# A four-layer graph network on one core: the third layer aggregates plain features by Strassen products and multiplies by its matrix afterwards

## The chip, the cores and the metric

The kernel runs on one core of a Trainium2 chip. The metric is the device time of one execution in microseconds (us). The median of three runs before the change is 2856.06 us (2855.82 to 2856.15). Engines are named as in the profile: PE (matrix engine; PEld is its weight load), DVE (vector), ACT (scalar), POOL (gpsimd) and SP (sync, which issues transfers). "Clock" is the share of its full clock that PE was granted.

## What is computed

A graph has 4096 nodes with 256 features each and one adjacency matrix (int32, symmetric in its pattern, with ones on the diagonal). Four layers follow one another, and each is wrapped as `x = layernorm(x + layer(x))`.

```
layer 0: additive attention, 4 heads of 64, leaky relu 0.2, softmax over neighbours, ELU
layer 1: 4-head dot-product attention over neighbours (Wq, Wk, Wv with biases)
layer 2: h = x @ W
         e[i,j] = leaky_relu(h[i]·a[:D] + h[j]·a[D:], 0.01), only where adj[i,j] > 0
         elu(softmax_j(e) @ h)
layer 3: cosine attention: unit vectors of x @ Wq.T and x @ Wk.T (128 wide), exp, mask, softmax,
         0.5 * (softmax @ x) + 0.5 * x
```

"Third layer" here is layer 2 of this list, the one with a single additive head. Two identities matter. Softmax times `h` is softmax times `x`, times `W`, so the matrix can come before or after the sum over neighbours. And the exponential of a leaky relu of a sum is the greater of two products of a factor of the row and a factor of the column, so no exponential is needed for each pair of nodes: before, the kernel writes it as `(relu(row * dst - 1) + 1) * mask`, up to factors that cancel in the softmax or are put into the values.

## The kernel before

All features stay in `X`, 32 tiles of 128 nodes (`NT`), each 256 wide. Attention is computed transposed: neighbours lie on the partitions, and a block of 512 nodes (`QW`; `NB` = 8 blocks, `QB` = 4 tiles in each) on the columns. Every layer loops over the blocks, and within a block over the neighbours. The orders of PE, and in layer 1 of DVE and ACT too, are those of the program text (`manual_schedule`); in the third layer only PE's order is fixed, and the framework's scheduler orders DVE and ACT.

Layer 1 (`multi_head_attention`) goes over 64 units of 64 neighbours in each block (`NH`). `scores` loads a mask on SP's queue for each four units, makes four 64x64-weight products into one of three `p` buffers in PSUM (L670), and exponentiates them on ACT (L672). `weights` multiplies with the mask on DVE (L682), from PSUM into one of eight `prob` buffers. The denominators are summed beside that: even units are added to `den` by POOL (L689), odd units by a DMA that accumulates, issued from POOL's queue (L695). `sums` is the product with the values (L703), three units later. The function `finish(b, j)` does a part of the finishing of the block before after unit j of the sums: it joins the three parts of `den` on DVE at j = 7 and 9 (L712), turns, divides, adds to `X`, takes mean and variance (j = 21 to 27) and the inverse root of the variance (j = 29 on DVE, `end_root` at j = 31 on POOL, L156 to L159), and scales the rows (`scale_row`, j = 35 to 41). The last block is finished by `tail`, inside the third layer.

The third layer (`additive_one`) first turns `X` block by block on PE (L118), projects with the matrix and the two attention columns (`additive_values`, L200), and keeps `V`, `src`, `dst` and a `row` of 4096 column factors; all this lies before and between the sums of block 0. For each tile of neighbours, `weights` makes `e` on ACT (L460) and `prob` on DVE (L462), with both inputs in SBUF. `sums` has four products of 128 weight columns of `prob` with the 257 columns of `V` (L468). A block's results are taken from PSUM by `take_all` (L474, L476); `outputs` and `add_elu` (L214 to L217) finish it over the next block, and `layernorm_block` with `lift=True` prepares the next layer. In the last block the cosine layer's `prepare` (L883 and on) turns and projects the finished blocks.

The last layer (`cosine_attention`) has scores (L941), exponentials (L945), mask products (L952) and mixes of weights (L954 to L957) for pairs of tiles, and already multiplies a 2x2 arrangement of half features and half blocks with seven products in place of eight (`product`, L966). `parts` joins the sum of one `acc` tile of four banks on ACT and DVE (L972 to L984) before the turns on PE (L992).

The function `turned_apart` turns a block by DVE's 32x32 transposes (L131) and a round trip through DRAM, without PE.

Of the kernel before, what the change touches and what calls it, by code (L numbers as in the profile page):

```python
# [9 lines left out]
FP = mybir.dt.float32  # L10
# [11 lines left out]
QB = 4  # L22
# [6 lines left out]
def kernel(  # L29
# [49 lines left out]
    X = feat.tile([P, NT, D + 1], FP, name="X")  # L79
    nc.vector.memset(X[:, :, D:], 2.0)  # L80
# [42 lines left out]
    def turned_apart(squares, far, part, to, eng):  # L123

        B = P // QB
        squares = squares.tile([P, QB, KC, P], FP, name="squares")
        far = far.tile([QB, B, QB, KC * P], FP, name="far")
        for c in range(KC):  # L130
            nc.vector.transpose(squares[:, :, c, :].rearrange("p q (k n) -> p k q n", n=B),  # L131
                                part(c).rearrange("p k (q f) -> p k q f", f=B))
        eng.dma_start(far.rearrange("a f q m -> (a f) (q m)"), squares.rearrange("p q c m -> p (q c m)"))
        for q in range(QB):
            eng.dma_start(to[q * B:(q + 1) * B], far[:, :, q, :].rearrange("a f m -> f a m"))
        return to.rearrange("p a (c m) -> p c a m", c=KC)

    def block_apart(sb, once, dr, b, eng):
        xT = sb.tile([P, KC * QW], FP, name="xT").rearrange("p (a m) -> p a m", a=QB)
        return turned_apart(once, dr, lambda c: X[:, b * QB:(b + 1) * QB, c * P:(c + 1) * P], xT, eng)  # L140
# [34 lines left out]

    def normalise(ys, mv, lift=False):
        v, r, n = begin_root(mv)
        end_root(v, r, n)
        if lift:

            nc.vector.tensor_tensor(v, v, r, OP.mult)
            nc.vector.tensor_tensor(mv[:, :, 0], mv[:, :, 0], v, OP.subtract)
        for k, y in enumerate(ys):
            scale_row(y, mv, r, k)
# [25 lines left out]
    def add_elu(o, b, k, mv):  # L210

        y = X[:, b * QB + k, :D]
        neg = fin1.tile([P, D], FP, name="neg")
# [6 lines left out]
    def additive_heads(a, H, slope, early, narrow, ahead):  # L220
# [7 lines left out]
        with ExitStack() as lay:  # L228
# [83 lines left out]
            def outputs(po, b, k):  # L312
                rden = fin.tile([P, H], FP, name="rden")
                nc.vector.reciprocal(rden, po[:, HC, ::G])
                o = fin.tile([P, D], FP, name="o")
# [3 lines left out]
                add_elu(o, b, k, mvs[b])  # L319

            def finish(b, j):
# [6 lines left out]
                if j in (4, 7, 10, 13):  # L328
                    k = (j - 4) // 3
                    outputs(pos[b, k], b, k)  # L330
# [67 lines left out]
        def tail(bank):  # L398
            b = NB - 1
            for k in range(QB):  # L400
                outputs(turned(bank, b, k), b, k)
# [3 lines left out]
    def additive_one(w_sb, slope, tail, op, follow):  # L405

        MJ = 2
        mvs, taken = {}, {}
        with ExitStack() as lay:
            keep = pool(lay, "gb_keep", 1)  # L410
            V = keep.tile([P, NT, D + 1], FP, name="V")
            src = keep.tile([P, NT, 1], FP, name="src")
            dst = keep.tile([P, NT, 1], FP, name="dst")
            row = keep.tile([P, N], FP, name="row")
            zp = pool(lay, "gb_z", 3)
            sb = pool(lay, "gb_sb", 2)
            xp = pool(lay, "gb_turn", 3)
            sq = pool(lay, "gb_squares", 1)
            far = pool(lay, "gb_far", 2, space=bass.MemoryType.DRAM)

            follow.turning = xp, sq, far
            mp = pool(lay, "gb_mask", 4)
            dr = pool(lay, "gb_dram", 2, space=bass.MemoryType.DRAM)

            ps = pool(lay, "gb_ps", 4, space=PSUM)
            pa = pool(lay, "gb_pa", 1, space=PSUM)
            edges = adjT.rearrange("(t p) i -> p t i", p=P)
            mask, acc, prob = {}, {}, {}
# [4 lines left out]
            def turn(b):  # L433
                return transposed_block(xp, bank, b)

            def project(b, xT, ks=range(QB)):
                groups = [(k, 1, bank().rearrange("p (n f) -> p n f", n=1)) for k in ks]
                additive_values(xT, b, groups, w_sb, V, src, dst, 1, slope)

            def fill_row(b):  # L440
                part = row[:, b * QW:(b + 1) * QW]
                if b > 1:

                    far = dr.tile([QB, P], FP, name="far")
                    nc.gpsimd.dma_start(far.rearrange("k p -> p k"), src[:, b * QB:(b + 1) * QB, 0])
                    nc.gpsimd.dma_start(part, far.rearrange("k p -> (k p)").unsqueeze(0).to_broadcast([P, QW]))
                    return
                pr = bank()
                for k in range(QB):
                    nc.tensor.transpose(pr[:, k * P:(k + 1) * P], src[:, b * QB + k, :].to_broadcast([P, P]), ident)  # L450
                nc.scalar.copy(part, pr)

            def weights(b, j):
                cols = slice(b * QW, (b + 1) * QW)
                m = b, j // MJ
                if j % MJ == 0:
                    mask[m] = mp.tile([P, MJ, QW], I32, name="mask")
                    nc.sync.dma_start(mask[m], edges[:, j:j + MJ, cols])
                e = sb.tile([P, QW], FP, name="e")
                nc.scalar.activation(e, row[:, cols], AF.Relu, bias=-1.0, scale=dst[:, j, :])  # L460
                prob[b, j] = zp.tile([P, QW], FP, name="prob")
                nc.vector.scalar_tensor_tensor(prob[b, j], e, 1.0, mask[m][:, j % MJ, :], OP.add, OP.mult)  # L462

            def sums(b, j):
                if j == 0:
                    acc[b] = [bank() if b % 2 else pa.tile([P, QW], FP, name=f"acc{k}") for k in range(QB)]
                for k in range(QB):
                    nc.tensor.matmul(acc[b][k][:, :D + 1], prob[b, j][:, k * P:(k + 1) * P], V[:, j, :],  # L468
                                     start=(j == 0), stop=(j == NT - 1))

            def take_all(b):
                for k in range(QB):
                    rden = fin.tile([P, 1], FP, name="rden1")
                    nc.vector.reciprocal(rden, acc[b][k][:, D:D + 1])  # L474
                    taken[b, k] = op.tile([P, D], FP, name="o")
                    nc.vector.tensor_scalar_mul(taken[b, k], acc[b][k][:, :D], rden)  # L476

            def outputs(b, k):
                if k == 0:
                    mvs[b] = fin.tile([P, QB, 2], FP, name="mv")  # L480
                add_elu(taken[b, k], b, k, mvs[b])
                if k == QB - 1:
                    layernorm_block(b, mvs[b], lift=True)

            def even_bank():
                n = next(even) % QB
                return pa.tile([P, QW], FP, name=f"acc{n}")

            even = itertools.count()
            units = [(b, j) for b in range(NB) for j in range(NT)]  # L490
            with tc.manual_schedule(engines={mybir.EngineType.PE}):
                xTs = {0: turn(0), 1: turn(1)}
                project(0, xTs[0])
                project(1, xTs[1], [0, 1])
                fill_row(0)
                project(1, xTs[1], [2, 3])
                for i in range(len(units) + 1):
                    if i < len(units):
# [691 lines left out]
```

## Time and profile before

| | us |
|---|---|
| median of three runs | 2856.06 |
| profiled execution: time | 2856.27 |
| profiled execution: span on the core | 2854.5 |
| PE busy | 2832.5 (99%) |
| DVE, ACT, POOL busy | 2168.0, 1653.4, 945.3 |
| layer 0 | 0 to 722.5 |
| layer 1: projections; blocks | to 809; to 1709.6 |
| third layer | to 2213 |
| cosine layer; end | to 2842; to 2854.5 |

The granted clock was 0.998 over the span. The span is the time from the first to the last instruction on the core; the device time is 1.8 us longer. The borders of the layers are read from the lines that PE works on. In the profile a group is one line, engine, operation and tile; "mean ns" is the mean length of one instruction, which for pipelined matmuls is longer than the distance from one start to the next. "Idle before" is the time in which the engine had nothing to do just ahead of that group, with what ended it.

### The profile page before, as it was taken

What the parts mean: (1) busy time and instruction counts of PE and PEld (TensorE: products, weight loads), DVE (VectorE), ACT (ScalarE), POOL (GpSimd) and SP (SyncE); (2) the same over time, 40 slices, a digit from 0 to 9 for tenths busy, and PEclk for the clock granted to TensorE, in tenths of its full rate; (3) what the DMA queues carried; (4) which work ended last, traced back from release to release, by engine and by line L of the source; (5) the groups of instructions that cost most, each with busy time, mean ns of one, the idle gap of its engine ahead of it and who ended that gap; (6) DMA issues with size and microseconds to landing.
All of it is one profiled execution on the core that took longest, in us unless ns stands there. A gap on an engine that the chain in (4) does not pass through costs nothing.

```text
span 2854.5 us, 50462 instructions
## 1 busy us (share of the span) xinstructions
PE 2832.5 (99%) x19905; PEld 1503.5 (53%) x19905; DVE 2168.0 (76%) x2913; ACT 1653.4 (58%) x2590; POOL 945.3 (33%) x705
## 2 busy tenths in 40 slices
PE   9999999999999999999999999999999999999998
PEld 4333333333543333333333338888888777777775
DVE  8899999999677777777777775565557966666665
ACT  8899999998256666666666664444445322222222
POOL 0001001010058889899899891000002000000000
PEclk9999999999999999999999999999999999999999
DMA  7566767665359899899899895655558544444441
GB/s 209 104 136 139 140 136 140 133 136 106 97 112 195 178 191 191 181 193 187 183 193 185 186 183 126 174 165 175 158 159 221 104 65 61 61 66 59 62 57 29
DMA packets 237088, 398.04 MB, mean 139 GB/s; under 512 B 20929, under 2 KB 121265, under 8 KB 235954
## 3 DMA queue, kind: packets, MB, share of 16 engines
q0 software_dynamic: 104320, 184.06, 40.5%
q1 hardware_dynamic: 132112, 210.36, 24.9%
q8 instruction: 156, 2.56, 0.4%
q14 instruction: 82, 0.67, 0.1%
q10 hardware_dynamic: 418, 0.40, 0.0%
HBM read 328.60 MB, written 32.58 MB: 127 GB/s over the span
## 4 chain that ended last, share of the span: by engine, by line
PE 97%; DVE 2%; ACT 0%; issue 0%; DMA 0%; ACTq 0%
PE acc L297 23%; PE p L670 15%; PE acc L703 15%; PE acc L966 13%; PE acc L468 8%; PE g L468 8%; PE p L941 3%; PE g L941 3%; PE g L585 2%; PE g L200 1%; PE pv L604 1%; PE acc L883 1%; PE acc L200 1%; PE g L118 1%; PE g L309 0%; DVE prob L952 0%
## 5 line engine op out<-in xcount | busy, mean ns | idle before, releaser
L682 DVE TENSOR_TENSOR prob<-p,mask 128x1024 f32<-128x1024 f32 x512 | 623.9, 1223 | 209.3 <-ACT p L672 203.2
L672 ACT ACTIVATE p<-p,shift 128x1024 f32<-128x1024 f32 x512 | 556.2, 1088 | 325.2 <-PE p L670 324.4
L297 PE MATMUL acc<-prob,V 128*32 128x512 f32 x6144 | 664.0, 592 | 1.2 <-DVE prob L287 1.2
L689 POOL TENSOR_TENSOR den<-den,prob 128x1024 f32<-128x1024 f32 x248 | 625.6, 2522 | 74.9 <-DVE prob L682 67.1
L284 ACT ACTIVATE prob<-row,dst 128x512 f32<-128x512 f32 x1020 | 633.2, 713 | 0.1
L287 DVE SCALAR_TENSOR_TENSOR prob<-prob,mask 128x2048 f32<-128x2048 f32 x256 | 582.5, 2287 | 24.2 <-ACT prob L284 21.5
L670 PE MATMUL p<-qT,kT 64*64 64x512 f32 x4096 | 532.3, 590 | 0.8 <-DVE prob L682 0.8
L703 PE MATMUL acc<-prob,V 64*64 64x512 f32 x4096 | 531.5, 589 | 0.0
L297 PEld LDWEIGHTS acc<-prob,V 128*32 128x32 f32 x6144 | 197.3, 110 | 453.0 <-issue 431.7
L91 POOL COPY tick<-prob 128x1 f32<-128x1 f32 x35 | 40.0, 1143 | 992.8 <-DVE prob L287 643.9
L460 ACT ACTIVATE e<-row,dst 128x512 f32<-128x512 f32 x256 | 183.9, 721 | 247.2 <-DVE prob L462 218.5
L703 PEld LDWEIGHTS acc<-prob,V 64*64 64x64 f32 x4096 | 155.9, 133 | 285.3 <-issue 278.1
L462 DVE SCALAR_TENSOR_TENSOR prob<-e,mask 128x512 f32<-128x512 f32 x256 | 177.2, 694 | 165.9 <-PE acc L468 88.5
L670 PEld LDWEIGHTS p<-qT,kT 64*64 64x64 f32 x4096 | 154.4, 133 | 277.3 <-issue 261.6
L952 DVE TENSOR_TENSOR prob<-prob,mask 128x1024 f32<-128x1024 f32 x128 | 156.4, 1222 | 165.9 <-ACT prob L945 165.8
L695 POOL DMA_DIRECT2D den<-prob x240 | 228.9, 954 | 14.7 <-DVE prob L682 6.7
L868 POOL DMA_DIRECT2D mask<-in_adjT x64 | 47.5, 742 | 538.7 <-DVE prob L952 424.8
L468 PE MATMUL acc<-V,prob 128*128 128x257 f32 x1024 | 225.1, 380 | 0.0
L468 PE MATMUL g<-V,prob 128*128 128x257 f32 x1024 | 223.7, 380 | 0.0
L468 PEld LDWEIGHTS g<-V,prob 128*128 128x128 f32 x1024 | 194.3, 190 | 27.7
L468 PEld LDWEIGHTS acc<-V,prob 128*128 128x128 f32 x1024 | 193.6, 190 | 27.6 <-issue 0.4
L966 PE MATMUL acc<-mix,mixed 128*128 128x256 f32 x768 | 206.9, 379 | 0.0
(199 smaller groups left out, 2520.8 us busy)
## 6 DMA issues: line engine op xcount, KB each, us to landing
mask<-in_adjT SPq DMA_DIRECT2D x256, 512.0 KB
den<-prob POOLq DMA_DIRECT2D x240, 512.0 KB, 5.1
mask<-edges SPq DMA_DIRECT2D x512, 64.0 KB
mask<-in_adjT POOLq DMA_DIRECT2D x64, 512.0 KB, 5.7
edges<-in_adj POOLq DMA_DIRECT2D x32, 512.0 KB, 10.1
far<-squares SPq DMA_DIRECT2D x16, 512.0 KB
den<-prob SPq DMA_DIRECT2D x16, 512.0 KB
row<-far SPq DMA_DIRECT2D x7, 1024.0 KB
```

What stands on the lines that cost most here:

```text
L284: nc.scalar.activation(z[:, h, :], r, AF.Relu, bias=-1.0, scale=dst[:, j, h:h + 1])
L287: nc.vector.scalar_tensor_tensor(z, z, 1.0, mask[m][:, j % MJ, :].unsqueeze(1).to_broadcast([P, H, QW]), OP.add, OP.mult)
L297: nc.tensor.matmul(acc[b][h * G:(h + 1) * G, n, :], part, prob[b, j][:, h, :], start=(j == 0), stop=(j == NT - 1))
L460: nc.scalar.activation(e, row[:, cols], AF.Relu, bias=-1.0, scale=dst[:, j, :])
L468: nc.tensor.matmul(acc[b][k][:, :D + 1], prob[b, j][:, k * P:(k + 1) * P], V[:, j, :], start=(j == 0), stop=(j == NT - 1))
L670: nc.tensor.matmul(p[c * d:(c + 1) * d, r, :], kT[half, c, at:at + d], qT[half, c, cols], start=True, stop=True)
L672: nc.scalar.activation(p, p, AF.Exp, bias=shift)
L682: nc.vector.tensor_tensor(z, p, mask[m][:, j % MJ, :].unsqueeze(1).to_broadcast([P, KC, QW]), OP.mult)
L689: nc.gpsimd.tensor_tensor(to, to, flat, OP.add)
L695: nc.gpsimd.dma_start(to, flat, accum_op=OP.add)
L703: nc.tensor.matmul(acc[b][c][r * d:(r + 1) * d, :], V[half, j, r * d:(r + 1) * d], prob[b, j][half, r, :], start=(j == 0), stop=(j == NH - 1))
L966: nc.tensor.matmul(acc[b][:, at, half * HW:(half + 1) * HW], w, a, start=(g == 0 and half == 0), stop=(g == NP - 1), skip_group_check=True)
```

## The change

The change rewrites the third layer, moves the making of its factors into layer 1, and shares the seven-product code with the cosine layer.

- A new class `Additive` holds the factors. `spread`, in layer 1's projections, copies the two attention columns (the matrix times the attention vector) over all partitions as `a_row`, takes their mean off, and takes the column mean off the matrix. `dots` makes both factors' exponents of one tile by a DVE multiplication with a sum. `factors` takes the exponentials and sends the row factors to DRAM. In layer 1's `finish`, `dots` stands at j = 43, 45, 47, 49, `factors` at 51.
- `lift_mean` (v·r and the mean minus it) is now done with the rows of layer 1, on POOL at j = 31.
- In the third layer nothing is turned or projected beforehand. `weights` goes by pairs of tiles: relu on ACT into PSUM (`r`), then add and mask on DVE into `z`, and for blocks 1 to 7 `mix_weights` (one DVE operation of 512 columns, two POOL operations of 256). `sums` has seven products of 128 weight columns of (mixed) features with 256 columns; block 0, during which the features are mixed, has the plain product with 512 columns. Four accumulators of one bank each replace the two sets of four.
- The sums are joined into four `quarters`, and `project` multiplies each tile with the matrix afterwards, during the next block (g = 2 to 8), followed by `take` (ACT) and `add` (DVE), the root at g = 11 and 12 (its end on POOL), and scaling on ACT at 13 and 14. The lifted rows are no longer written over `X` (later blocks still read it) but saved to DRAM from ACT's queue, and loaded again in the last block.
- PE's, DVE's and ACT's orders are now all fixed in the third layer. The cosine layer's `prepare` is spread over the blocks in smaller steps instead of lying in the last block; some of its operations go to POOL and ACT.
- The tail of layer 1 is a generator with small steps, run twice after each pair of tiles in block 0. Its first steps join `den` on DVE where POOL did.
- In the cosine layer the accumulator is four tiles of one bank, and the joining is split into `first_half` (three accumulators) and `second_half`.
- The column of twos at the end of `X` is dropped.

```diff
+    def mix_weights(s, z, eng):
+        nc.vector.tensor_tensor(s[:, :2, :], z[:, 0, :].rearrange("p (h i) -> p h i", h=2), z[:, :, HW:], OP.subtract)
+        eng.tensor_tensor(s[:, 2, :], z[:, 0, :HW], s[:, 1, :], OP.subtract)
+        eng.tensor_tensor(s[:, 3, :], z[:, 1, :HW], s[:, 2, :], OP.subtract)
+
+    def first_half(c, one, acc):
+        nc.scalar.copy(one, acc[3][:, :HW])
+        nc.vector.tensor_tensor(c[:, :2, :], one.unsqueeze(1).to_broadcast([P, 2, HW]),
+                                acc[0].rearrange("p (h i) -> p h i", h=2), OP.add)
+        nc.vector.tensor_tensor(c[:, 2, :], c[:, 1, :], acc[1][:, :HW], OP.add)
+        nc.vector.tensor_tensor(c[:, 3, :], c[:, 2, :], acc[1][:, HW:], OP.add)
+
+    def second_half(c, acc):
+        nc.vector.tensor_tensor(c[:, 1:3, :], c[:, 1:3, :], acc[2][:, :HW].unsqueeze(1).to_broadcast([P, 2, HW]), OP.add)
+        nc.vector.tensor_tensor(c[:, 1, :], c[:, 1, :], acc[2][:, HW:], OP.add)
+
+    class Additive:
...
+        def dots(self, t):
+            for n in range(2):
+                junk = fin1.tile([P, D], FP, name="neg")
+                nc.vector.tensor_tensor_reduce(junk, X[:, t, :D], self.a_row[:, n, :], 1.0, 0.0, OP.mult, OP.add,
+                                               self.dot[:, t, n:n + 1])
+
+        def factors(self, b):
...
+            nc.scalar.activation(src, s, AF.Exp, scale=1.0 - self.slope)
+            nc.scalar.activation(self.dst[:, t], d, AF.Exp)
+            nc.scalar.activation(self.own[:, t], d, AF.Exp, scale=self.slope)
+            nc.vector.tensor_scalar_mul(self.less[:, t], self.own[:, t], -1.0)
+            far = self.rows[b] = self.far.tile([QB, P], FP, name=f"far2_{b}")
+            nc.scalar.dma_start(far.rearrange("k p -> p k"), src)
...
     def additive_one(...):
-                xTs = {0: turn(0), 1: turn(1)}
-                project(0, xTs[0])
...
-                e = sb.tile([P, QW], FP, name="e")
-                nc.scalar.activation(e, row[:, cols], AF.Relu, bias=-1.0, scale=dst[:, j, :])
-                nc.vector.scalar_tensor_tensor(prob[b, j], e, 1.0, mask[m][:, j % MJ, :], OP.add, OP.mult)
+                    r = pr.tile([P, QW], FP, name="r")
+                    nc.scalar.activation(r, ga.row_of(b), AF.Relu, bias=ga.less[:, j:j + 1], scale=ga.dst[:, j:j + 1])
+                    nc.vector.scalar_tensor_tensor(z[:, n, :], r, ga.own[:, j:j + 1], mask[:, n, :], OP.add, OP.mult)
+                if b:
+                    s = mix[b, g] = zp.tile([P, 4, HW], FP, name="mix")
+                    mix_weights(s, z, nc.gpsimd)
...
-                for k in range(QB):
-                    nc.tensor.matmul(acc[b][k][:, :D + 1], prob[b, j][:, k * P:(k + 1) * P], V[:, j, :],
+                if b:
+                    for n in range(7):
+                        product(acc[b], prob[b, g], mix[b, g], mixed[g // 2][:, g % 2], g, n)
+                else:
+                    for j in range(2 * g, 2 * g + 2):
+                        for c in range(KC):
+                            nc.tensor.matmul(acc[b][c], X[:, j, c * P:(c + 1) * P], prob[b, g][:, j % 2, :],
...
+            def project(bank, b, k):
+                po = drawn[b, k] = bank()
+                for c, quarter in enumerate(quarters(kept[b], k)):
+                    nc.tensor.matmul(po[:, :D + 1], quarter, w_sb[:, c, :D + 1], start=(c == 0), stop=(c == KC - 1))
...
+                elif g == 12:
+                    v, r, n = roots[b]
+                    end_root(v, r, n, nc.gpsimd)
+                    nc.gpsimd.tensor_tensor(v, mvs[b][:, :, 0], r, OP.mult)
+                    nc.gpsimd.tensor_scalar(v, v, -1.0, 1.0, OP.mult, OP.add)
+                elif g in (13, 14):
...
+                        nc.scalar.activation(y, y, AF.Identity, bias=v[:, k:k + 1], scale=r[:, k:k + 1])
...
     multi_head_attention, finish:
                     end_root(*roots[b], nc.gpsimd)
+                    lift_mean(mvs[b], *roots[b][:2], nc.gpsimd)
...
+                elif j in (43, 45, 47, 49):
+                    ga.dots(b * QB + (j - 43) // 2)
+                elif j == 51:
+                    ga.factors(b)
+                elif j == 57 and b == 0:
+                    ga.row(b, nc.sync)
```

## The prediction

> **What bounds the kernel now.** I read the busy times first, then the chain that ended last, then one row of stages.
>
> ```profile
> PE 2832.5 (99%) x19905; PEld 1503.5 (53%) x19905; DVE 2168.0 (76%) x2913; ACT 1653.4 (58%) x2590; POOL 945.3 (33%) x705
> PE 97%; DVE 2%; ACT 0%; issue 0%; DMA 0%; ACTq 0%
> 809.00:1709.60 900.60, 899.75 (x8389) 320.44 (x8388) 686.69 (x672) 566.53 (x547) 804.57 (x523) 1.00 0.90 186
> 1734.00:2213.00 479.00, 479.00 (x2232) 419.64 (x2231) 288.98 (x649) 213.90 (x465) 27.32 (x48) 1.00 0.62 169
> ```
>
> The last two are the stretch of layer 1's blocks and most of the third layer (bounds, length, then busy us and instructions of PE, PEld, DVE, ACT, POOL; clock, DMA share, GB/s). PE is busy throughout at full clock, and 97% of the ending chain is PE: a matmul removed from the third layer is time saved, if the others keep up. In layer 1 PE is just as full, but POOL is at 804.6/900.6 = 89% beside it: that matters below.
>
> The chain by time prices PE (start us, us, work, instructions; one f32 matmul is two instructions):
>
> ```profile
> 1804.11 55.51 PE g L468 x256
> 1859.62 55.51 PE acc L468 x256
> ...
> 2142.39 3.45 PE acc L883 x16
> ```
>
> A 257-column instruction takes 55.51/256 = 0.217 us, a 256-column one 3.45/16 = 0.216, a 512-column one 0.43 (the cosine scores L941: 0.86 for two). The "mean ns" of the groups (L468: 380) counts overlapped pipeline time, so it isn't used.
>
> [...] 109 ns at 128 columns, 216 at 256, 429 at 512; so columns decide.
> [...] POOL and DVE met here:
>
> ```profile
> 1721.57 2.54 POOL L712 TENSOR_TENSOR den<-den 128x1024 f32<-128x1024 f32 x1 [7.52 <-DMA den<-prob]
> ...
> 1722.13 2.52 DVE L462 SCALAR_TENSOR_TENSOR prob<-e,mask 128x512 f32<-128x512 f32 x1 [0.25 <-ACT e L460]
> ```
>
> L462 normally takes 0.69; it ended 0.54 after POOL did. L682, with one input in PSUM, keeps to 1.22 beside POOL all through layer 1.
>
> **The change, part by part** (against the profiled execution: span 2854.5, time 2856.27; the median, 2856.06, is 0.2 lower).
>
> 1. *PE, third layer.* Removed: L468 8 × 55.51 = 444.1; the projections of L200, 128 instructions × 0.217 = 27.8; 64 turns of X, 128 × 0.109 = 14.0; the 8 turns of L450, 1.7: 487.6. Added: block 0, 64 matmuls of 512 columns = 128 × 0.429 = 54.9; blocks 1 to 7, 16 pairs × 7 products × 2 = 224 instructions × 0.216 = 48.3 each, 338; the projection afterwards, 64 matmuls of 257 = 27.8; `spread`, in layer 1's prologue, 4 turns and 2 matmuls, 1.7: 422.4. **−65**.
>
> 2. *Do the others keep up in the third layer?* One pair of tiles has 7 × 2 × 0.216 = 3.02 us of PE. DVE: two products with the mask 2 × 0.69, one mix over 512 elements 0.69 (L954), so 2.1 us; over a block with finishing and the cosine's turns I count about 44 of PE's 52 us. The mask product reads `r` in PSUM, so POOL can't hold it up. POOL: two adds over 256 columns; L689 takes 2.36 us for 1024, 2.3 ns a column, so about 0.75 with a start of 0.2: 1.5 of 3.02. PE runs two pairs behind, so a chain of some 4.2 us (relu, two products, mix, two adds) has 6.04. Hidden; POOL would have to take over 1.7 us an add to stall PE. At a block's g = 12 (its 12th pair), ACT's scalings (queued ahead of the next relus) wait for ten small POOL operations (0.2 us, 0.28 start to start; they stand at L156 to L159 in layer 1 now), 2.8 us, behind the two adds: estimated 1 us of stall in each of 6 blocks, **+6 (0 to +14)**. ACT's store of a finished block (g = 15) and the cosine's scalings cost nothing: ACT has some 32 us of work (32 × 0.72 and the rest) in 52.
>
> 3. *Start of the third layer.* Before, PE turned and projected from 1709.7 while the masks came (the first issued at 1709.8, a 512 KB mask in about 3 us). Now nothing covers them; their buffers lie over `kT`, free after the last scores, so they may be issued some 3 us earlier. Layer 1's end (join on DVE behind the den DMA, row sums, a copy on ACT, the turn) now stands between fewer matmuls. **+3 (+1 to +8)**. The rows go on SP at g = 11, behind masks that have four buffers: nothing waits.
>
> 4. *Handover to the cosine, and its blocks.* The cosine's score buffers wait for the last projections' banks: +0.5 (0 to +2). Splitting its sum into `first_half` and `second_half` lets PE go on before the whole sum is joined; before, PE waited at each block:
>
> ```profile
> PEld g L992 <- DVE u L984: 9.3, 7, 1.3
> ```
>
> In start-to-start gaps that is 0.67 a block × 7: **−4.7** (−5.5 to −2), with 0.5 at the end: −5.
>
> 5. *The dot products in layer 1.* `ga.dots` puts two reductions over 256 elements a tile on DVE, with X and `a_row` both in SBUF, after the mask product of unit 46, 48, 50, 52 of a block: even units, each of which releases POOL's add at the same moment.
>
> ```profile
> L689 POOL TENSOR_TENSOR den<-den,prob x248: 2344/2360/3214, 814.9 to 1707.1; 128x1024 f32<-128x1024 f32 x124
> L682 DVE TENSOR_TENSOR prob<-p,mask 128x1024 f32<-128x1024 f32 x512 | 623.9, 1223 | 209.3 <-ACT p L672 203.2
> ```
>
> POOL's add (min/median/max ns) starts 0.16 us after the mask product's end[...]; the longest, 3.21, had DVE's L712 (also two SBUF inputs) just ahead of it. So the first reduction, which needs nothing new, gets in (to about 0.35); POOL waits and goes next; the second reduction writes the same `neg`, so it waits for the first's end[...]. A tile then takes DVE 0.35 + 2.2 (POOL) + 0.4 = **2.9 us** in place of 1.0 (2 × 0.42, the price of L957, and readout).
> Queued behind it on DVE are the next mask products; each frees a score buffer `p` that PE waits for. What it costs: a unit has 1.72 us of PE and 1.22 of L682, so DVE gains 0.5 a unit. Over the four tiles the delay grows to 4 × 2.9 − 3.65 = 7.95. The score buffers `p` (three) give 1.5 of slack: the product ends 3.45 after its scores start, and the buffer is due at 5.15. Left: 6.4 a block, × 7 blocks = **+45**. Unblocked (1.0): 0. The trace shows no such reduction: if it runs at half rate (0.68[...]) beside the wait, 3.4 a tile: 8.5 a block, +60. I take 2.9.
> The factors (ACT, three small exponentials and a DMA issue, once a block), the lift on POOL (2 more operations of 0.28 among eight `prob` buffers) and layer 1's last tile in the tail: 0, because ACT is 63% busy there and POOL's backlog has buffers; without cover, some 0.7 × 7 = 5.
>
> Sum: −65 + 6 + 3 + 0.5 − 5 + 45 = −15.5: 2840.8 profiled.
>
> **Rivals.**
> *A, the forecast:* the second reduction waits for POOL at nearly every tile: **2840**, own range 2826 to 2856.
> *B[...]:* the second reduction is taken before POOL's request is granted. For: [...]all 14 L712 on DVE kept to 1216 ns. Against: L462 at 1722.13, which arrived later and waited to the end. Then part 5 is 0: **2795** (2786 to 2808). If some tiles escape, 2800 to 2830.
> *C, slower:* a tile's dots hold DVE past the point where part 5 eats all else: 7 × (4x − 5.15) = 60.5 gives x = 3.45 us. Half-rate reductions with the wait come just to it, and both reductions waiting (2 × 2.2 + 0.8 = 5.2) go far over (+109): **2865 to 2905**. For: POOL's starts jitter (2344 to 3214). Against: the first is in the queue, ready, before POOL's semaphore fires.
> *D, a matrix gain that isn't there:* POOL's adds exceed 1.7 us[...]; at 2.3 the third layer follows POOL and loses all of part 1. L689 speaks against it; I count it with C.
>
> **Chances.** A 0.51, B and partly escaped tiles 0.32, C and D 0.17. A measurement tells about 0.2% (5.7 us) from no change. A's upper end and C's lower make "same" 0.06; faster 0.80, slower 0.14. The range runs from B's lower part to C's nearer end, 2788 to 2866.
>
> **What would show it.** In the changed trace: a third-layer block of 52 us on PE (48.3 and its projection) in place of 55.5; in layer 1, pairs of reductions where the second takes over 2 us and PE gaps near units 48 to 56 of about 6 us a block; POOL adds of some 2.5 there. If reductions are all under 0.7 and layer 1 keeps its 900 us, B holds; if both of a pair exceed 2 us, C. PE gaps every pair in the third layer would refute part 2; a first sum later than 5 us after the last layer 1 matmul, part 3.

## The result, and the profile after

The changed kernel takes 2885.33 us (median of 4 runs, 2885.03 to 2888.58) against 2856.11 before: a ratio of 1.0105, 95% interval 1.0087 to 1.0122. It is slower, by about 1%; 2840 with a gain was forecast. Its profiled execution has a span of 2883.7.

The stages of both traces, cut at the first or last matmul of the same lines:

| stage | before, us | after, us | difference | forecast |
|---|---|---|---|---|
| layer 0 | 723.1 | 723.9 | +0.8 | 0 |
| layer 1, projections | 85.9 | 88.5 | +2.6 | +2 |
| layer 1, blocks | 900.6 | 946.3 | +45.7 | +45 |
| third layer | 503.7 | 488.2 | -15.4 | -57 |
| cosine layer and end | 641.2 | 636.9 | -4.4 | -5 |

So the cost in layer 1 came as computed, and the gain of the third layer did not. The busy times of the page, and the rows of stages (bounds, length, busy us of PE, PEld, DVE, ACT, POOL with instructions, clock, DMA share, GB/s) for layer 1's blocks, the third layer's block 0 and its blocks 1 to 7:

```profile
PE 2798.0 (97%) x19489; PEld 1427.6 (50%) x19489; DVE 2307.1 (80%) x3010; ACT 1698.3 (59%) x2641; POOL 1118.9 (39%) x1009
...
812.40:1758.70 946.30, 906.64 (x8389) 317.68 (x8388) 769.31 (x791) 570.92 (x570) 807.05 (x537) 1.00 0.89 177
1758.70:1823.70 65.00, 61.00 (x165) 27.59 (x161) 49.52 (x107) 27.83 (x44) 5.93 (x12) 0.95 0.72 198
1823.70:2246.90 423.20, 396.95 (x1786) 336.36 (x1784) 321.24 (x555) 231.46 (x484) 196.58 (x321) 1.00 0.62 186
```

Before, PE was busy in every microsecond of the third layer. Now it idles 423.2 - 396.9 = 26.3 us in blocks 1 to 7 and some 40 in layer 1's blocks, where as many matmuls are issued as before (8389). The DVE's busy time in layer 1 grew by 83 us, far more than 56 reductions of 0.41 and their readouts explain.

In layer 1, the timeline around one tile's two reductions (start us, us, engine, line; L817 is the mask product, L824 POOL's add; DVE and POOL are separate answers):

```profile
1011.46 0.41 DVE L501 CUSTOM_DVE_ANT_0 neg<-X,a_row 128x256 f32<-128x256 f32 x1
1011.80 0.08 DVE L501 DVE_READ_ACCUMULATOR2_ANT dot<- 128x1 f32 x1
1011.91 2.45 DVE L501 CUSTOM_DVE_ANT_0 neg<-X,a_row 128x256 f32<-128x256 f32 x1
1014.29 0.08 DVE L501 DVE_READ_ACCUMULATOR2_ANT dot<- 128x1 f32 x1
```

```profile
1011.69 2.39 POOL L824 TENSOR_TENSOR den<-den,prob 128x1024 f32<-128x1024 f32 x1
```

The first reduction takes 0.41 us; POOL's add starts beside it, and the second one, the same operation, takes 2.45 and ends 0.28 after POOL. At all 28 tiles of layer 1 the second takes 2.45 to 3.16 and ends 0.28 to 0.29 after POOL's add; in the third layer's tail, where POOL makes no such add, all eight take 0.42 to 0.43. The distances of layer 1's scores show the price: 1.72 us for a plain unit, but four longer ones a block behind the reductions, one of 2.6 to 3.9 and three of 3.3 to 3.9, which makes 6.0 to 7.6 us a block.

In the third layer, what PE waited for in blocks 1 to 7 (us in total, times, longest; and, beside it, DVE's and ACT's waits over one block, 1936.93 to 1998.36):

```profile
PE g L1033 <- ACT sq L1037: 9.3, 12, 1.1
PE acc L444 <- DVE quarters L450: 9.0, 6, 1.7
PE acc L444 <- POOL mix L435: 4.7, 8, 0.8
PE acc L444 <- ACT one L449: 1.9, 5, 0.4
PE acc L444 <- DVE quarters L458: 1.0, 5, 0.2
```

```profile
DVE prob L554 <- POOL mix L436: 6.5, 4, 1.6
DVE prob L554 <- ACT r L553: 5.9, 2, 3.2
DVE prob L554 <- POOL mix L435: 1.5, 1, 1.5
```

```profile
ACT e L591 <- DVE rden L589: 14.4, 4, 4.0
ACT r L553 <- DVE prob L554: 7.1, 8, 4.8
ACT sq L1037 <- PE g L1033: 2.8, 3, 1.3
ACT rows L1046 <- POOL r L169: 1.8, 1, 1.8
ACT r L159 <- DVE v L180: 1.6, 1, 1.6
```

Three things stop PE: the squares that ACT makes between PE's matmuls (L1033 and L1037), the mix near a block's end, and the joining of the block's sums (L449, L450, L458). A full block takes 61.4 us where PE has 55.3 of work. DVE and ACT are not full, 46 and 34 us of 61, but they wait for each other in turn: ACT's queue holds the next relus (L553) behind an operation that needs DVE (L591), POOL (L1046) or PE (L1037), and DVE waits for the relus. The four waits that DVE's first row puts down to POOL end 0.03 us after POOL's add, but also 0.09 after ACT's relu, so the name in the row doesn't settle it; h1b below, which moves L591, bears on it.

At the start of the third layer PE stands 3.5 us for the first masks and then runs at half speed for some 5 us: the first 512-column instructions follow each other at 0.85 us, where 0.43 is usual (the granted clock is 0.50 from 1761.2 to 1768.0, and 0.95 over block 0's row).

```profile
1762.30 9.93 PE L568 MATMUL acc<-prob,X 128*128 128x512 f32 x16 [3.48 <-DVE prob L554]
```

### The profile page after: what moved, and what is told of

The parts are those of the page before. It is cut to its first block, busy times and chain, and to the rows that moved or that the text cites. A ratio compares the mean times of both kernels' runs of the same rounds, so it can differ in the third digit from the quotient of the medians.

```text
span 2883.7 us, 50258 instructions
## 1 busy us (share of the span) xinstructions
PE 2798.0 (97%) x19489; PEld 1427.6 (50%) x19489; DVE 2307.1 (80%) x3010; ACT 1698.3 (59%) x2641; POOL 1118.9 (39%) x1009
## 5 line engine op out<-in xcount | busy, mean ns | idle before, releaser
L817 DVE TENSOR_TENSOR prob<-p,mask 128x1024 f32<-128x1024 f32 x512 | 620.3, 1221 | 171.7 <-ACT p L807 160.9
L824 POOL TENSOR_TENSOR den<-den,prob 128x1024 f32<-128x1024 f32 x248 | 635.9, 2564 | 51.2 <-DVE prob L817 41.4
L805 PE MATMUL p<-qT,kT 64*64 64x512 f32 x4096 | 538.7, 592 | 39.6 <-DVE prob L817 39.6
L444 PE MATMUL acc<-mix,mixed 128*128 128x256 f32 x1440 | 391.4, 381 | 5.7 <-POOL mix L435 4.7
L444 PEld LDWEIGHTS acc<-mix,mixed 128*128 128x128 f32 x1440 | 272.2, 190 | 48.1 <-POOL mix L435 7.9
L554 DVE SCALAR_TENSOR_TENSOR prob<-r,own,mask 128x512 f32<-128x512 f32 x256 | 179.7, 743 | 103.7 <-POOL mix L436 42.6
L444 PE MATMUL acc<-prob,X 128*128 128x256 f32 x960 | 251.2, 381 | 10.8 <-DVE quarters L450 9.0
L444 PEld LDWEIGHTS acc<-prob,X 128*128 128x128 f32 x960 | 181.0, 190 | 96.5 <-issue 63.1
L1088 ACT ACTIVATE prob<-p 128x512 f32<-128x512 f32 x144 | 86.0, 598 | 220.8 <-PE p L1084 204.4
L1088 ACT ACTIVATE prob<-g 128x512 f32<-128x512 f32 x112 | 66.7, 596 | 195.5 <-PE g L1084 195.5
```

What stands on the lines that cost most here:

```text
L444: nc.tensor.matmul(acc[at][:, half * HW:(half + 1) * HW], w, a, start=(g == 0 and half == 0), stop=(g == NP - 1), skip_group_check=True)
L554: nc.vector.scalar_tensor_tensor(z[:, n, :], r, ga.own[:, j:j + 1], mask[:, n, :], OP.add, OP.mult)
L805: nc.tensor.matmul(p[c * d:(c + 1) * d, r, :], kT[half, c, at:at + d], qT[half, c, cols], start=True, stop=True)
L817: nc.vector.tensor_tensor(z, p, mask[m][:, j % MJ, :].unsqueeze(1).to_broadcast([P, KC, QW]), OP.mult)
L824: nc.gpsimd.tensor_tensor(to, to, flat, OP.add)
```

## The experiments

All times are medians in us, ratios are against the kernel before (2856.1). The edits are cut to the lines that matter; `...` marks what is left out.

**Layer 1: e1_dots_apart.** Each reduction after an even unit of its own.

```diff
...
-                elif j in (43, 45, 47, 49):
-                    ga.dots(b * QB + (j - 43) // 2)
-                elif j == 51:
+                elif j in (43, 45, 47, 49, 51, 53, 55, 57):
+                    n = (j - 43) // 2
+                    ga.dots(b * QB + n // 2, (n % 2,))
+                elif j == 59:
...
```

> The two reductions of a tile stand after different even units (j = 43, 45, ... 57; factors at 59, first row at 61); nothing else changes. If layer 1 lost its time to the second reduction[...] (2.45 us against 0.41 for the first), a single reduction after an even unit always goes ahead of POOL's add: all near 0.41, layer 1's blocks back at 900 us, total 2885 - 45 = 2840. If the loss comes from DVE having more work there (56 more reductions, wherever they stand), layer 1 keeps at least half of its 45 us: 2862 or more.

Measured 2849.07, ratio 0.9973 (0.9964 to 0.9983): 36 us less than the change, with as many reductions.

```profile
L501 DVE CUSTOM_DVE_ANT_0 neg<-X,a_row x64: 415/416/1308, 1005.8 to 1764.5; 128x256 f32<-128x256 f32 x64
```

Their median is 416 ns (minimum 415, maximum 1308), and layer 1's blocks take 904.3 in place of 946.3. So it isn't the load but the place. One that stands alone, near the end of layer 1, falls between two of POOL's adds (DVE and POOL are separate answers):

```profile
1710.18 0.41 DVE L501 CUSTOM_DVE_ANT_0 neg<-X,a_row 128x256 f32<-128x256 f32 x1
```

```profile
1707.01 3.05 POOL L824 TENSOR_TENSOR den<-den,prob 128x1024 f32<-128x1024 f32 x1
...
1710.42 2.84 POOL L824 TENSOR_TENSOR den<-den,prob 128x1024 f32<-128x1024 f32 x1
```

It starts 0.12 us after the one ends and 0.24 ahead of the next, and takes 0.41. What made others as long as 1.3 us is not shown by these rows. The missing 6 us are at the third layer's start (f1).

**e2_own_junk.** Separate tiles for the unused products.

```diff
-                junk = fin1.tile([P, D], FP, name="neg")
+                junk = fin1.tile([P, D], BF, name=f"neg{n}")
```

> The two reductions of a tile write their unused products to two tiles (bf16, for room) in place of one, and stay together. If POOL gets in because the second waits for the first's write of the same tile, the second now follows at once: 0.42 us, total about 2840. If POOL is granted the ports at the end of the first instruction in any case, the second still takes about 2.45 and the total stays at 2885 (within 5).

One run, 2885.65: no change.

```profile
L501 DVE CUSTOM_DVE_ANT_0 neg<-X,a_row x64: 406/426/3277, 1005.9 to 1798.4; 128x256 bf16<-128x256 f32 x64
```

The longest still takes 3.28 us, and none of layer 1's 45 us comes back. So the shared output isn't what lets POOL in: the second reductions stay late though they no longer wait for the first ones' writes. One rival stays here: the short readout of the sum (0.08 us) stands between the two reductions in this run too, and may be the gap that POOL uses. The change's own third layer speaks against it. There L601 follows L600 without a readout, both with two SBUF inputs, and POOL's mix add (L435) starts during L600:

```profile
1970.57 0.42 DVE L600 SCALAR_TENSOR_TENSOR e<-e,h 128x256 f32<-128x256 f32 x1
1971.02 0.83 DVE L601 TENSOR_TENSOR y<-X,e 128x256 f32<-128x256 f32 x1
```

```profile
1970.79 0.78 POOL L435 TENSOR_TENSOR mix<-prob,mix 128x256 f32<-128x256 f32 x1 [2.31 <-DVE mix L434]
```

L601 takes 0.83 us at all 28 tiles where POOL's mix adds are at work beside it, and 0.42 at the four where they aren't. But L601 reads what L600 writes; no run has a pair with neither a readout nor a dependency.

**f1_late_rows.** e1, with the store of block 6's row moved behind layer 1.

```diff
-            nc.scalar.dma_start(far.rearrange("k p -> p k"), src)
+            self.held[b] = src
+            if b != NB - 2:
+                for n in sorted(self.held):
+                    far = self.rows[n] = self.far.tile([QB, P], FP, name=f"far2_{n}")
+                    nc.scalar.dma_start(far.rearrange("k p -> p k"), self.held.pop(n))
```

> As e1_dots_apart, but the row of block 6 is sent to DRAM with that of block 7, in the third layer, in place of some 4 us before layer 1's end. In e1 PE stood 8.6 us at the third layer's start (4 in the change), and the DMA moved 10 to 40 GB/s there while it was busy. If the row's 512 packets of 4 bytes hold up the first masks, the start is back at 4 us and the total falls from 2849 to about 2842. If the masks are late because layer 1's transfers are now closer together (its pace is 1.72 again), nothing changes: 2849.

Measured 2843.52, ratio 0.9952 (0.9937 to 0.9967): 5.5 below e1. From layer 1's end to the first seven-product matmul it takes 66.4 us, in e1 74.8, in the change 65.0. In e1 a transfer of 512 values of 4 bytes was issued some 4 us before layer 1's end and 0.5 us before the first mask, and the masks came late: from 1716.6 to 1721 the DMA moved 9 to 40 GB/s. Whether its small pieces or only its place did that, the run doesn't separate.

**e3_squares_after.** The squares behind all the matmuls, on the change itself.

```diff
                     nc.tensor.matmul(prs[k // 2][:, k % 2, :, :], xT[:, c, k], w_sb[:, c, :], ...
+            for k in range(QB):
                 for n in range(2):
                     sq = in_.tile([P, P], FP, name="sq")
```

> In the third layer's preparation of the cosine layer, ACT's squares stand after all 16 matmul instructions in place of between them (as before the change). PE's two waits for ACT there (0.88 and 0.94 us a block, 6 blocks) go: 2885 - 11 = 2874, if that time isn't taken back at the next wait. If DVE and ACT are the ones that are late in the third layer, PE only waits 1.8 us more at the mix and at the block's end: 2885 to 2880.

Measured 2877.89, ratio 1.0071 (1.0054 to 1.0087): 7.4 less than the change, of the 11 that these waits hold when counted from start to start. The wait is gone; the mix wait grew (0.88 to 1.06 us a block), and the granted clock over the execution fell from 0.997 to 0.996.

**e4_muls_later.** The preparation one pair earlier, its scalings one pair after their root.

```diff
             end_root(v, r, QB * 2, nc.gpsimd)
+            yield
...
-                        if b > 1 and g in (3, 5, 10, 11, 12, 13, 14, 15):
+                        if b > 1 and g in (3, 5, 9, 10, 11, 12, 13, 14, 15):
```

> The preparation's matmuls and root start one pair earlier (g = 9, 10, 11), and ACT's eight scalings stand one pair after the root's end on POOL (g = 12), so ACT doesn't wait for POOL's ten small operations. Theory: that wait makes ACT's relus and DVE late, and DVE is still late at the block's end, so both the mix wait (0.87) and the block's end (0.53 + 1.85 + 0.37) go: 3.6 x 6 = -22, 2863. Rival: the block's end is DVE's own order (the joining stands behind the next pairs' products and the turns), and only the mix wait goes: -5, 2880.

Measured 2906.20, ratio 1.0168 (1.0152 to 1.0183): 21 slower than the change, against both. At g = 9 ACT takes a finished tile just ahead of the squares, and PE's wait for the squares rose from 1.8 to 3.1 us a block. The 1.85 for L450 stayed. That is some 8 of the 21 us. The granted clock over the execution was 0.993, against 0.997 in the change; 0.004 of 2905 us, some 12, is my estimate of what that cost. This run couldn't tell its two theories apart, since it put a new wait in.

**f2_sq_lag.** f1 with the squares of e3, and PE three pairs behind. To make room, the masks have three buffers in place of four, and `e` and `h` one in place of two.

```diff
-            mp = pool(lay, "gb_mask", 4)
-            zp = pool(lay, "gb_z", 3)
+            mp = pool(lay, "gb_mask", 3)
+            zp = pool(lay, "gb_z", 4)
...
-            sb = pool(lay, "gb_sb", 2)
+            sb = pool(lay, "gb_sb", 1)
...
-            LAG = 2
+            LAG = 3
```

> f1 with the squares after the matmuls, and PE three pairs behind the weights in place of two (four buffers of weights; three of masks and one of e, h to make room). Theory: in the third layer ACT and DVE are late by some 3 us where ACT stands behind PE's projection and POOL's root; one more pair (3.0 us) hides it, so the waits for the mix (0.9) and most of the block's end (2.75) go besides the 1.8 at the squares: 6 x 5 below f1, about 2812. Rival: the block's end is DVE's order, as the joining stands behind the next block's products, and these can't start before their buffers are free: only 6 x 2.7 below f1, 2826.

Measured 2838.59, ratio 0.9939 (0.9922 to 0.9955). f1 with the squares alone was not run; 2843.5 less e3's 7.4, an estimate of 2836, stands for it. The mix wait is gone, and what it gave came back at the joining (PE's waits in the blocks):

```profile
PE acc L444 <- ACT one L449: 9.7, 5, 2.2
PE acc L444 <- DVE quarters L450: 9.6, 6, 1.7
```

More lead alone doesn't help here: the joining stands in ACT's and DVE's queues behind the products of the pair `LAG` ahead. That the fewer buffers played no part is not shown by this run; h3b has the same ones.

**f3_root_dve and f4_root_join.** f1 with the squares of e3 and both roots' ends on DVE; then also the joining first:

```diff
-            end_root(v, r, QB * 2, nc.gpsimd)
+            end_root(v, r, QB * 2)
...
+                        if g == NP - 1 and i < len(units):
+                            weights(*units[i])
```

> f1 with the squares after the matmuls, and both roots' ends at g = 12 on DVE in place of POOL (ten operations of 0.16 us there, 1.6 in all). Theory: ACT's scalings no longer wait behind POOL's adds and root (from 1986.0 to 1989.2 in the change's trace), so relus and products come some 2 us earlier: the mix wait goes and the block's end falls from 2.75 to about 1: 6 x (1.8 + 0.9 + 1.7) = 26 below f1, 2815. Rival: DVE is the late engine; then the mix wait and the block's end stay, and only the squares' 1.8 (less 0.2 at the mix) is gained: 6 x 1.6 below f1, 2831.

> f3 with the joining of a block's sums ahead of the next pair's products on ACT and DVE (it stood behind them). If the block's end waits because of that order, PE's waits for the joining (ACT copy, L450, L458) vanish; the products come later instead, and PE waits for that pair's mix up to 1.5 us: about 1.2 a block less than f3, 7 below it. If the block's end was gone already in f3, it gets 6 x 1.3 worse.

Measured 2850.85, ratio 0.9979 (0.9970 to 0.9988), and 2849.19, ratio 0.9973 (0.9962 to 0.9983). f3 is 7 slower than f1 and both theories missed it. PE's waits in f3, then f4:

```profile
PE acc L444 <- DVE prob L557: 13.2, 6, 2.3
PE acc L444 <- POOL mix L435: 4.7, 8, 0.9
PE acc L444 <- DVE quarters L450: 4.4, 4, 1.7
```

```profile
PE acc L444 <- DVE prob L557: 13.3, 6, 2.3
PE acc L444 <- POOL mix L435: 11.2, 17, 1.7
```

The roots' ends now stand on DVE behind a pair's products. In one block ACT's scalings wait 4.1 us for them (1.8 for POOL in the change), the next relus stand behind the scalings, and DVE's products (L557) come late. But PE's waits are no longer than in f1, 23 us against 26, so they don't explain the 7 us. What fell is the granted clock. Blocks 1 to 7 in f1, then f3 (the clock is the third number from the end):

```profile
1782.60:2205.50 422.90, 397.04 (x1785) 336.26 (x1784) 320.65 (x555) 231.58 (x483) 196.93 (x321) 1.00 0.60 186
1782.20:2211.30 429.10, 405.25 (x1785) 342.93 (x1784) 335.32 (x617) 230.17 (x483) 182.75 (x256) 0.97 0.60 183
```

Over the whole executions it was 0.997 in the change and in f1, 0.994 in f2, and 0.993 in f3, f4 and e4. Where the change's clock is 0.50, its matmuls take twice as long (0.85 us in place of 0.43 for 512 columns, 0.43 in place of 0.22 for 256), so I put f3's 7 us down to the clock. That is an estimate: 0.03 of 429.1 us is up to 13, and less where PE waits anyway. With two pairs of lead, the joining moved ahead frees the joining, and the wait turns into one for the mix (4.7 to 11.2).

**f6b_lag_join.** f2 and the joining first.

> f2_sq_lag with the joining of a block's sums ahead of the next pair's products on ACT and DVE. In f2 PE waits for nothing but the joining (ACT's copy 2.1, DVE's L450 1.85 a block), because ACT and DVE have the relus and products of the third pair of the next block ahead of it, and these could only start when their buffers came free. Theory: moved ahead, the joining follows PE's last sums at once, and the third pair still has two pairs (6 us) until it is needed: about 4 x 6 = 24 below f2, 2815. Rival: ACT and DVE are simply late there, and PE waits for the third pair's mix instead: at most 6 below, 2832.

Measured 2831.38, ratio 0.9915 (0.9900 to 0.9930), 7 below f2: nearer the rival.

```profile
PE acc L444 <- DVE quarters L450: 5.6, 6, 1.0
PE acc L444 <- ACT one L449: 5.0, 6, 1.1
PE g L1039 <- ACT h L595: 3.2, 2, 2.9
```

The waits for the joining (L449 and L450) fell from 19.3 to 10.6 us over the blocks, none turned into mix waits (that of 3.2 us for ACT's L595 is new, at the preparation's matmuls), but ACT and DVE are still late when the joining comes.

**h1b_take_later and h2b_one_step.** What ACT waits for, one step later: first e and h, then also the roots and the scalings (both on f1 with the squares of e3).

```diff
...
                 if g in (4, 6, 8, 10):
+                    draw(sb, b, g // 2 - 2)
                     add(b, g // 2 - 2)
...
```

```diff
-                    roots[b] = begin_root(mvs[b])
+                    v = roots[b] = fin.tile([P, QB], FP, name=f"v{QB}")
+                    nc.vector.tensor_scalar_add(v, mvs[b][:, :, 1], EPS)
...
-                    v, r, n = roots[b]
+                    v, r, n = roots[b] = roots[b], first_root(roots[b], QB), QB
...
```

> f1 with the squares after the matmuls, and ACT's two operations of a finished tile (e, h) one step later, behind the next relus. In the change ACT waits four times 3.6 us a block for DVE's reciprocal, which stands behind a pair's products and mix, and the next relus stand behind ACT's two operations: DVE then idles 1.6 us, four times a block. Theory 1 (DVE and ACT work in series over the whole block and their rate is the limit): 6 us a block come back, about 2812. Theory 2 (PE only suffers from what is late after g = 10, where ACT waits for PE's projection and all earlier lead is lost): no more than the squares' own gain, 2836.

> h1b and, after g = 10, every ACT operation one step behind what it waits for: the roots' ACT part at g = 12 behind the relus, the scalings at 13 (the turned rows and their transfers one step later). So ACT's queue holds no relu behind a wait for DVE or POOL. Theory 2 of h1b: DVE's waits for ACT after g = 10 (5.9 + 1.5 us a block) go, and with them the mix wait (0.9 to 1.1) and most of the 2.75 at the block's end: some 18 below h1b, about 2818. If the block's end comes from the place of the joining behind the next products: only the mix wait goes, 5 to 6 below h1b.

Measured 2832.96, ratio 0.9911 (0.9894 to 0.9928), and 2827.15, ratio 0.9898 (0.9883 to 0.9913). h1b is near theory 2: with L591 moved, DVE's four waits of 6.5 us over a block became one:

```profile
DVE prob L557 <- POOL mix L436: 1.7, 1, 1.7
```

So they hung on ACT's order. But DVE's waits over the block only moved: 13.8 us in all, against 13.9 in the change, with 7.4 for the relus in place of 5.9. PE waits at the same two places as before. In h2b the mix wait (4.5 us) is gone, as its rival said:

```profile
PE acc L444 <- DVE quarters L450: 9.9, 5, 2.0
PE acc L444 <- ACT one L449: 3.2, 5, 0.6
```

Its median is 5.8 lower than h1b's, which is what the rival said too, but the intervals of the two overlap. The joining (L449 and L450) still costs 13.1.

**h3b_step_lag_join.** h2b with three pairs of lead and the joining first.

> h2b with PE three pairs behind and the joining first. If the three causes (ACT's waits, two pairs of lead, the order at the block's end) are all there is, the third layer's blocks come down to PE's own 55.3 us and the total to f1 less 6 x 6.2: about 2806. Stalls that stay would be new ones.

Measured 2822.76, ratio 0.9881 (0.9866 to 0.9895): faster than both kernels, though not by what was expected. Its rows of stages (layer 1's blocks, block 0, blocks 1 to 7; of an execution of 2818.52) and PE's waits in the last:

```profile
812.50:1714.20 901.70, 900.31 (x8389) 320.12 (x8388) 719.41 (x791) 570.16 (x570) 805.45 (x538) 1.00 0.93 186
1714.20:1782.10 67.90, 61.38 (x164) 28.03 (x161) 50.26 (x107) 27.82 (x44) 4.66 (x11) 0.95 0.64 180
1782.10:2181.00 398.90, 390.27 (x1786) 336.82 (x1784) 320.52 (x551) 231.78 (x483) 201.96 (x322) 1.00 0.67 198
```

```profile
PE acc L444 <- DVE quarters L450: 4.6, 5, 1.2
PE g L1048 <- ACT h L599: 2.7, 1, 2.7
PE acc L444 <- DVE quarters L458: 1.0, 5, 0.2
```

PE's waits in blocks 1 to 7 fell from 26 to 8 us with the same work on every engine, at a mean clock of 1.00; a full block takes 57.3, and the seven 398.9 in place of 423.2. So most of the third layer's loss was order and lead. Alone, more lead (f2) and the joining first (f4) only moved the wait, and the later queue (h2b) took one of PE's two waits away. Some 2 us a block at the joining remain, against the forecast.

**k1_tail_later.** h3b with layer 1's tail begun later in block 0.

```diff
-                            for _ in range(2):
+                            for _ in range(3 if g > 1 else 0):
```

> h3b with the steps of layer 1's tail begun two pairs later in the third layer's block 0 (three a pair from g = 2, in place of two a pair from g = 0). In h3b PE waits 3.7 us for the joined denominators (L874 <- DVE L861), which stand on DVE behind masks still on their way, and then runs some matmuls at half the clock. If the tail only comes too early, that wait goes: 3 to 5 us below h3b, about 2818. If DVE is late there whatever the order (masks), PE waits as long for the third pair's products instead: unchanged, 2823.

Measured 2822.14, ratio 0.9879 (0.9863 to 0.9896): unchanged. The wait for the joined denominators only moved (3.7 to 4.7 us). DVE's waits between layer 1's end and block 1, in h3b and in k1:

```profile
DVE prob L557 <- DMA mask<-in_adjT: 11.9, 4, 6.4
```

```profile
DVE prob L557 <- DMA mask<-in_adjT: 12.2, 4, 6.7
```

What the start costs (67.9 us in h3b, PE 61.4 of them busy, at a mean clock of 0.95) goes back, in both orders, to masks that are not there yet. That is read from these rows; no run brought the masks earlier.

## Why the prediction was wrong

- **Part 5, the reductions, was right in its cost.** 45.7 us against 45, or 6.0 to 7.6 a block against 6.4; a tile's pair holds DVE 2.9 us. Its reason for POOL's turn (the second reduction waits for the shared `neg`) was wrong: e2 took that away, and nothing changed. That the outcome held all the same was luck. By its own figures the slack is 5.15 − 3.45 = 1.7, not 1.5, which makes it 44. Rival B and the half-rate case fell as well: 0.41 us for an unblocked reduction, where the half-rate case had 0.68.
- **Part 4, the cosine layer, was right:** -4.4 against -5. PE's waits for the join at each block are gone there, and 1.7 us of projections came in from the third layer.
- **Part 1 had a count wrong.** A turn is one instruction, not two: the chain by time of the kernel before has, at the third layer's start, two blocks of 8 turns as 16 instructions:

```profile
1709.72 1.90 PE g L118 x16
```

  So 64 turns are 7.0 us, not 14.0, and the 8 of L450 are 0.9: the matmuls removed are 479.8 us, and part 1 is -57, not -65. This alone is 8 us.
- **Part 2 failed, and this decided the sign.** It divided busy time by pair (2.1 us of DVE and 1.5 of POOL in 3.02 of PE) and called the rest hidden, with 6 us at g = 12 as the only stall. This step failed: busy shares that fit do not make the work hidden. ACT and DVE take turns: an ACT queue with a wait in it holds back the relus, those the products, and a joining that is written behind the products of two pairs ahead comes when both are done. PE's waits there are 26.3 us, besides 3.4 us at half clock from the end of one of them on. The mechanism named for g = 12 was there (L1046 waits 1.8 us for POOL's root, and the mix wait follows), with 0.9 us a block (from start to start), near the 1 it was sized at; the squares between PE's own matmuls (9.3 us) and the joining (11.9 us) were not in the sum at all. I had counted the handover at a block's end at nothing without naming what hides it. h3b, with the same instructions in another order and more lead, gets 24 of the 38 us back that blocks 1 to 7 take beyond PE's own work. The part also looked only at the mask product when it asked whether POOL can hold DVE up. That one (L554) did keep to 0.71 to 0.75 us at all 72 places beside POOL's mix adds; DVE's L601, with two SBUF inputs, takes 0.41 us more beside them at 28 tiles.
- **Part 3 was low:** the start lost about 7 us against 3, inside its range of 1 to 8, 2.9 of it by matmuls at half clock.
- With these terms the sum closes. PE's own work in the third layer is 479.8 + 20.7 (preparation) + 3.1 (layer 1's tail and a centring) = 503.6 us before, which is what it took, and 421.1 + 20.7 + 3.1 = 444.9 after (1.7 of it, the last eight projection instructions, runs beyond the stage's border), where it took 488.2. Of these 43.3 us PE is idle for 30.3 (488.2 less 457.9 busy, from the rows above); the other 13 to 15 are matmuls that follow each other more slowly. Some 4.5 of it lie in the two stretches at half clock, most of the rest at the waits: the last matmul before one counts with its whole length (0.38 us in place of 0.22), and the first after it is followed by the next after 0.32. I had counted 9.5. So 2840.8 + 7.8 (turns) + 33.8 = 2882.4, and 3.1 from small differences elsewhere: 2885.5, the profiled time.
- Rival C had the sign but not the cause: it wanted more than 3.45 us a tile in layer 1, or POOL over 1.7 us an add (measured 0.72). The chance of 0.14 for slower was too small because both unknown sums, layer 1 and the third layer, stood with only one of them bounded widely.

Left open: the 0.8 to 1.2 us a block at L450 that h3b keeps, how the first masks could come earlier, and after which of PE's pauses the clock is halved: in the change the same 1.7 us at L450 came just before it in one block and not in four others.

## What to carry to other kernels

A kernel that is 99% one engine has hidden its others behind that engine's work; when a change takes 12% of that work away in a stage, read for every other engine not its busy share but the longest chain from one engine's queue to the next and back, block ends included. Where an engine's order is fixed, look for operations that wait for work of the same step, and try them one step later (h2b lost its mix wait so), but expect the wait to move until lead and order are right together (h3b). Look also for two DVE instructions with two SBUF inputs each in a row where an instruction of POOL starts beside the first: here the second took 2.45 us in place of 0.41, and placed one at a time (e1) they cost layer 1 3.7 us in place of 45.7.

## What the runs showed of the hardware

- DVE beside POOL: of two DVE reductions in a row, with an add of POOL that starts beside the first, the second takes 2.45 to 3.16 us in place of 0.41 at all 28 tiles of layer 1 in the change, and ends 0.28 to 0.29 after the add. Without a dependency between the two (e2) the total stays at 2885.65. L601 behind L600, with no readout between, takes 0.83 in place of 0.42 at all 28 tiles beside POOL's mix adds. With one input in PSUM, L554 keeps to 0.71 to 0.75 at the 72 places beside these adds. That POOL gets its turn after one DVE instruction is my reading of these times. What grants a turn, which e2's expectation calls "the ports", no trace shows.
- PE at half speed: 853 ns from one 512-column instruction to the next in place of 429, after the 3.5 us at the third layer's start, and 427 in place of 216 for 256 columns, after a wait of 1.7 us at L450. In the change the granted clock is 0.50 from 1761.2 to 1768.0, from 2061.5 to 2065.0 and in the last 10 us, behind the last layer; after four other waits of 1.7 us at L450 it stays at 1.00. A wait of PE may thus go with a loss beyond its length: f3 has 3 us less of waits than f1 in blocks 1 to 7 and takes 6 more, at a clock of 0.97 in place of 1.00.
- A transfer of 512 pieces of 4 bytes, issued 0.5 us ahead of the first 512 KB mask, went with 5.5 us more of the total (e1 against f1).
